# An attention kernel in quarter products: v joins the stream, first factors move into the attention

## The chip, the cores and the metric

The kernel runs on one core of a Trainium2 chip. A core has engines with a queue of instructions each: TensorE (PE, with weight loads listed as PEld), VectorE (DVE), ScalarE (ACT), GpSimd (POOL), and SyncE (SP), which only issues DMAs here. Engines wait for each other by semaphores. PE reads on-chip SBUF and writes PSUM; DVE and ACT read both, POOL only SBUF. The metric is device time in microseconds of one launch, all numbers in float32. The time before is 3212.28 us, the median of 3 runs (3211.11 to 3212.94).

## The reference

Two layers are applied one after the other to x of shape (8, 512, 32, 32): 8 images, C = 512 channels, N = 1024 tokens. A layer, for one image:

```python
xn = group_norm(x) * scale + bias          # 8 groups in layer 0, 32 in layer 1
q, k, v = split(qkv_w @ xn + qkv_b)        # (512, 1024) each, 8 heads of 64 channels
attn = softmax(q.T @ k / 8, over the keys) # per head, 1024 x 1024
out = proj_w @ (v @ attn.T) + proj_b + x
```

## The kernel before

The work is done in 16 units (u = 0 to 15): 8 images of layer 0, then 8 of layer 1. Layer 0 stores to mid in DRAM, from where layer 1 loads. The whole is an order written out by hand: each engine executes its instructions in program order, and hooks (lists of small steps, called `at("v", 6, ...)` or found by a step's number) say between which products a step is issued.

A unit has these stages on PE:

1. v (make_values): Winograd's form of Strassen's product, 7 outer products instead of 8, each of two 256-row chunks by direct matmuls: 56 matmuls of 128x256, tokens on the partitions. A float32 matmul is two instructions, each with a weight load, so 112.
2. q, k (make_pairs) and the projection of the unit before (project), in one stream (class Stream): here each of the 7 outer products is again done in Winograd's form, by 7 quarter products of 128x128 by 128x256. That is 49 matmuls, 98 instructions, for each of q, k and the projection. ACT copies the partial sum to the next quarter ("seed") and the seventh quarter product to SBUF ("late"); DVE finishes each outer product into running sums p1, u2, u3 and into the results; POOL adds the late part. The accumulators are two pairs of PSUM banks (apair), used in turn, with the other half of PSUM (sbank) for the partial sums.
3. The attention: 8 chunks (4 pairs of heads, 2 halves of the queries) of 8 steps each, s = 0 to 63. A step is 4 score matmuls of 64x64 tiles, exp on ACT, 4 matmuls with v, and on DVE one addition into the sums of p. Per chunk the sums are transposed and reduced on DVE, collected by small DMAs, inverted, spread by DMA (rb), and ao is multiplied by them (divide). There is no subtraction of a maximum.

A Winograd product needs left factors (of the weights, made once and stored as images in DRAM, loaded per unit in 7 pieces) and right factors of x. The class Right makes these: `mix(0..3)` makes the outer factors 5, 6, 4 and 7 by one DVE subtraction each, and `quarter` makes the inner factors t1, t2, t4 and b22 - b12 of one or two outer factors. For v only the outer factors are needed, so the inner ones are made by POOL during v. Their rooms are parts of the tiles for k, which are free then, and of others.

During the attention, the next unit's x is normalized in place. The function at_step is called behind each step with its number s. Its last part is one chain in which at most one arm runs in a step:

```python
if s == plan["norm"][0]:
    aggregate()
...
elif s in plan["apply"]:
    apply(*divmod(plan["apply"].index(s), NH))
elif s in (6 * NT + 2, 7 * NT + 3):
    right.mix(s // NT - 6)
```

NT is 8, NH 2, CC 4. In units other than 0 the plan is USUAL, whose apply steps are `[c * NT + t for c in range(2, 2 + CC) for t in (4, 6)]`; in unit 0 it is LATE, with 32, 33, 36, 38, 39, 41, 43, 44.

Since the softmax subtracts no maximum, the kernel guards itself: okay collects on DVE, with two instructions per pair of heads, whether all softmax sums lie between SUM_MIN = 2^-20 and SUM_MAX = 2^60, and asum whether ao is finite. At the end verdict reduces both over each partition, a matmul with ones counts the partitions in order, and the program reads this flag. If it is under 128, general_path (from line 1137) computes the whole output again, from x, in a loop over the 8 images with two layers each. It works plainly: for each of 64 blocks of 128 queries of a layer two matmuls of 512 columns for the scores, the maximum (line 1286), exp (1289), reciprocal and scaling (1291, 1292), 8 transposes on PE (1296), two copies from PSUM (1297), and per two blocks 8 matmuls with v of 256 columns (1303); before that 32 matmuls of 512 columns for v (1240) and 64 for q and k (1258), behind it 32 for the projection (1313). Scores, exponentials, transposed blocks and small results have two buffers each.

Of the kernel before, what the change touches and what calls it, by code (L numbers as in the profile page):

```python
# [11 lines left out]
F32 = mybir.dt.float32  # L12
I32 = mybir.dt.int32
AF = mybir.ActivationFunctionType
ALU = mybir.AluOpType
# [3 lines left out]
P = 128  # L19
# [13 lines left out]
def fast_path(ctx, tc, x, qkv_wT, proj_wT, vecs, groups, out, flag):  # L33
# [21 lines left out]
    def pool(name, bufs, **kw):  # L55
# [29 lines left out]
    okay = const.tile([P, 2 * BL], F32, name="okay")  # L85
# [6 lines left out]
    ot = aopool.tile([P, 3, 2, FD], F32, tag="ot", name="ot")  # L92

    images = [
        {
            sel: mids.tile([P, 7, FD if sel == "v" else 7 * P], F32, tag=f"i{sel}{l}", name=f"i{sel}{l}")
# [89 lines left out]
    def store_image(l, sel, left):  # L186
        to = images[l][sel]
        nc.sync.dma_start(to[:, :, :FD], left.block)
        if sel != "v":
            nc.sync.dma_start(to[:, :, FD:], left.made)  # L190

    def load_image(l, sel, slot, k):
        image = images[l][sel]
        return nc.sync.dma_start(slots[slot][:, k - 1, : image.shape[2]], image[:, k - 1, :])

    class Right:
# [24 lines left out]
        def quarter(self, pair, rooms, engine):  # L221
            v = self.views[pair[0]]
            t1, t2, t4 = rooms
            b11, b12, b21, b22 = (v[:, :, c, q, :] for c in range(2) for q in range(2))
            for i, k in enumerate(pair):
                self.inner[k] = {
                    1: b11[:, i], 2: b21[:, i], 3: b22[:, i], 7: b12[:, i],
                    5: t1[:, i], 6: t2[:, i], 4: t4[:, i],
                }
# [3 lines left out]
                partial(sub, b12, b22, b12),  # L233
# [162 lines left out]
    class Stream:  # L396
# [10 lines left out]
        def product(self, a, b, keep, finish):  # L407
# [6 lines left out]
            def part(j, dst, tile_name, bank, start=False):  # L414
                on(
                    "PE",
                    nc.tensor.matmul(dst, a[j], b[j], start=start, stop=j != 1, skip_group_check=True),  # L417
                    tile_name, bank,
                )
# [35 lines left out]

    def sum_steps(l, bias, name, early=None):
# [3 lines left out]
        def p1(main, m, late):  # L460
            t = st["p1"] = accpool.tile([P, 2, FD], F32, tag="acc", name=f"p1_{name}")
            on("DVE", nc.vector.tensor_scalar_add(t[:, 0, :], main[:, 0, :], vec[:, l, bias, 0:1]), m, 0)
# [14 lines left out]
        def u3(main, m, late):  # L477
            t = st["u3"] = accpool.tile([P, 2, FD], F32, tag="acc", name=f"u3_{name}")
            for i in range(2):
# [16 lines left out]
    def make_pairs(stream, w, sel, bias, left, early, hook):  # L496
# [32 lines left out]
        for k in ORDER:  # L529
# [7 lines left out]
            stream.product(left.quarters(k), w.right.inner[k], k == 3, finish)  # L537

# [67 lines left out]
    def make_values(w, left, banks, hook, between=None, behind=None):  # L606
# [3 lines left out]
        w.v = vpool.tile([P, NT, C], F32, tag="v", name=f"v_{u}")  # L610
        w.last["v"] = []
# [18 lines left out]
        run(steps[:6])  # L630
        if between is not None:
            between()
        run(steps[6:])
        if behind is not None:
            behind()
# [57 lines left out]
    def attention(w, at_step):  # L693
        u = w.u
        n_chunks = CC * NH
# [3 lines left out]

        def scores(s):  # L700
            c, t = divmod(s, NT)
            pr, qh = divmod(c, NH)
            if s < 6:
                bank = (*sbank, apair[1])[s % 3]
                before = state["exp"][s - 3 : s - 2] if s >= 3 else []
            elif s == n_steps - 1:
                bank = apair[0]
                before = state["free"][0]
            else:
                bank = sbank[s % 2]  # L710
                before = [state["exp"][s - (3 if s < 8 else 2)]]
            if s < 3:
                before = before + [i for i, _, _ in seen[("s0", "s1", "a1")[s]]]
# [17 lines left out]
        def products(s):  # L731
# [3 lines left out]
            banks = abank[2 * (c % 2) : 2 * (c % 2) + 2]  # L735
# [3 lines left out]
            if s == 0:  # L739
                before += w.last["v"] + [i for i, _, _ in seen["a0"]]  # L740
# [26 lines left out]
        def evacuate(c):  # L767
            pr, qh = divmod(c, NH)
            banks = abank[2 * (c % 2) : 2 * (c % 2) + 2]
            tmp = tmps[:, c % 2, :]  # L770
            i0 = nc.scalar.copy(tmp, banks[0])  # L771
# [8 lines left out]
        def reduced(c):  # L780
# [7 lines left out]
            if qh == NH - 1:  # L788
                lt = small.tile([BL, P // BL - 1, 2 * BL], F32, tag="lt", name=f"lt_{u}_{pr}")
                for k in range(1, P // BL):  # L790
                    nc.sync.dma_start(
                        lt[:, k - 1, :], red[k * BL : (k + 1) * BL].rearrange("i j h f -> i (j h f)")
# [3 lines left out]
        def reciprocals(pr):  # L796
            def work(name):
                return small.tile([BL, 2 * BL], F32, tag=name, name=f"{name}_{u}_{pr}", bufs=1)

            lt = state["lt"]  # L800
            one, two, tot, rows, rec = map(work, ("one", "two", "tot", "rows", "rec"))
            nc.vector.tensor_add(
                one, state["red"][:BL].rearrange("i j h f -> i (j h f)"), lt[:, 0, :]
            )
            nc.vector.tensor_add(two, lt[:, 1, :], lt[:, 2, :])
            nc.vector.tensor_add(tot, one, two)
            nc.vector.transpose(rows, tot)
            nc.vector.reciprocal(rec, rows)
            ok = okay[:BL]
            nc.vector.scalar_tensor_tensor(ok, tot, SUM_MAX, ok, ALU.is_le, ALU.mult)  # L810
            nc.vector.scalar_tensor_tensor(ok, tot, SUM_MIN, ok, ALU.is_ge, ALU.mult)
# [29 lines left out]
        for s in range(n_steps):  # L841
# [15 lines left out]
            summed(s, p)  # L857
# [3 lines left out]
        for h in range(NH):  # L861
            add_bias(CC - 2, h)
        transposed(n_chunks - 1)
        reduced(n_chunks - 1)
# [4 lines left out]

        w.finish = [partial(reciprocals, CC - 1), partial(divide, CC - 1), bias_last]  # L870
# [6 lines left out]
    nc.vector.memset(okay, 1.0)  # L877
# [33 lines left out]
    for u in range(2 * B):  # L911
        w = Unit()
        w.u, w.right, w.last, w.ready = u, right, {}, {}
# [11 lines left out]
        for sel in "qk":  # L925
            pairs = [
                qkpool.tile([P, 2, N], F32, tag=f"{sel}{r}", name=f"{sel}_{u}_{r}") for r in range(2)
            ]
            setattr(w, sel + "p", pairs)
            setattr(w, sel, [pairs[pr // 2][:, pr % 2, :] for pr in range(CC)])  # L930
# [18 lines left out]
        at("v", 1, make_rooms, partial(right.mix, 3))  # L949
# [448 lines left out]
```

## Time and profile before

| what | us |
|---|---|
| time, median of 3 | 3212.28 |
| the profiled execution | 3212.51 |
| its span | 3210.7 |
| PE busy | 3195.5 |
| DVE busy | 2773.0 |
| ACT busy | 1892.3 |
| POOL busy | 930.4 |
| the attention of unit 7 | 110.2 |
| v of unit 7 | 24.7 |
| q, k and projection of unit 7, together | 63.5 |

The page's busy times are sums over the execution; the span runs from the first to the last instruction. PE's share is 100%, but matmuls are pipelined and their ends modelled, so that a busy PE isn't PE at its peak. The prediction also uses three other views: busy time of each engine in a given stretch, the timeline (instructions in order of time, merged), and groups of instructions by line. The granted TensorE clock was 0.999 on average.

### The profile page before, as it was taken

How to read it: one execution, taken by the hardware profiler on the slowest of the kernel's cores; microseconds unless marked ns; L12 is line 12 of the kernel's file. 1: busy time of each engine (PE TensorE's matmuls, PEld its weight loads, DVE VectorE, ACT ScalarE, POOL GpSimd, SP SyncE). 2: the span in 40 equal slices, each digit the busy share in tenths (PEclk: the TensorE clock that was granted, in tenths of full speed). 3: DMA queues.
4: the chain of work that ended last, by engine and by line, in shares of the span. 5: the costliest groups of instructions: out<-in, count | busy, mean ns of one | idle time of the engine just before them, and what ended most of it. 6: DMA issues, size and time to landing. Idle time of an engine off the chain costs nothing.

```text
span 3210.7 us, 59813 instructions
## 1 busy us (share of the span) xinstructions
PE 3195.5 (100%) x23012; PEld 2023.7 (63%) x23012; DVE 2773.0 (86%) x3315; ACT 1892.3 (59%) x3077; POOL 930.4 (29%) x619
## 2 busy tenths in 40 slices
PE   9999999999999999999999999999999999999999
PEld 7466584765847658476584755747557485674843
DVE  7988988989899898888988889898888988989877
ACT  3656746466465665746657465574655746557464
POOL 5133060330604306043150421504224042240520
PEclk9999999999999999999999999999999999999999
DMA  5334242442534314233142332423323233232311
GB/s 197 109 108 131 79 159 96 132 131 93 160 105 128 120 45 157 74 108 127 43 162 68 107 124 61 143 70 122 108 79 126 74 119 106 86 130 74 123 64 49
DMA packets 151361, 344.84 MB, mean 107 GB/s; under 512 B 27168, under 2 KB 40992, under 8 KB 151072
## 3 DMA queue, kind: packets, MB, share of 16 engines
q1 hardware_dynamic: 150784, 340.81, 33.2%
q8 instruction: 187, 3.06, 0.4%
q14 instruction: 102, 0.84, 0.1%
q10 hardware_dynamic: 288, 0.13, 0.0%
HBM read 282.29 MB, written 57.02 MB: 106 GB/s over the span
## 4 chain that ended last, share of the span: by engine, by line
PE 94%; DVE 3%; issue 1%; POOL 0%; ACT 0%; DMA 0%; SPq 0%; DVEq 0%; POOLq 0%; ACTq 0%
PE a L746 26%; PE s L718 25%; PE s L417 18%; PE a L417 13%; PE a L394 6%; PE s L394 5%; DVE acc L765 1%; PE a L718 1%; PE s L672 0%; PE a L672 0%; DVE tr L777 0%; DVE acc L763 0%; DVE red L785 0%; DVE ao L772 0%; DVE xt L217 0%
## 5 line engine op out<-in xcount | busy, mean ns | idle before, releaser
L726 ACT ACTIVATE p<-s 128x1024 f32<-128x1024 f32 x976 | 997.6, 1024 | 522.7 <-PE s L718 495.4
L746 PE MATMUL a<-p,v 64*64 64x512 f32 x8192 | 1102.3, 589 | 0.0
L718 PE MATMUL s<-q,k 64*64 64x512 f32 x7808 | 1060.8, 590 | 0.0
L765 DVE TENSOR_TENSOR acc<-acc,p 128x1024 f32<-128x1024 f32 x768 | 938.3, 1222 | 77.9 <-ACT p L726 34.6
L746 PEld LDWEIGHTS a<-p,v 64*64 64x64 f32 x8192 | 385.1, 132 | 494.2 <-ACT p L726 348.3
L718 PEld LDWEIGHTS s<-q,k 64*64 64x64 f32 x7808 | 388.1, 133 | 426.9 <-issue 426.9
L422 ACT COPY a<-s 128x256 f32<-128x256 f32 x1308 | 465.8, 357 | 282.3 <-PE s L417 202.4
L947 POOL TENSOR_TENSOR k<-xn 128x512 f32<-128x512 f32 x16 | 20.3, 1269 | 1337.0 <-DVE xn L217 1337.0
L434 ACT COPY late<-s 128x256 f32<-128x256 f32 x327 | 121.7, 372 | 179.9 <-PE s L417 178.8
L394 PE MATMUL a<-w,xn 128*128 128x256 f32 x768 | 178.2, 382 | 0.5 <-DVE v L623 0.5
L832 ACT ACTIVATE ao<-ao,vec 128x512 f32<-128x512 f32 x128 | 88.4, 715 | 143.9 <-DVE ao L825 143.7
L394 PEld LDWEIGHTS a<-w,xn 128*128 128x128 f32 x768 | 144.6, 190 | 31.8 <-issue 12.2
L763 DVE TENSOR_TENSOR acc<-p,p 128x1024 f32<-128x1024 f32 x128 | 152.5, 1192 | 9.4 <-ACT p L726 9.4
L777 DVE STREAM_TRANSPOSE tr<-acc 128x1024 f32<-128x1024 f32 x128 | 158.0, 1235 | 0.0
L785 DVE TENSOR_REDUCE red<-tr 128x32 f32<-128x1024 f32 x128 | 154.3, 1206 | 0.6
L417 PE MATMUL s<-xn,w 128*128 128x256 f32 x492 | 146.8, 380 | 1.2 <-POOL xn L947 1.2
L417 PE MATMUL s<-k,w 128*128 128x256 f32 x492 | 146.4, 379 | 0.0
L417 PE MATMUL a<-xn,w 128*128 128x256 f32 x492 | 146.4, 379 | 0.0
L772 DVE TENSOR_TENSOR ao<-a,tmp 128x512 f32<-128x512 f32 x128 | 88.1, 688 | 61.4 <-ACT tmp L771 61.2
L417 PE MATMUL a<-xt,w 128*128 128x256 f32 x462 | 137.5, 379 | 0.0
L288 POOL TENSOR_TENSOR y<-var,half 128x4 f32<-128x4 f32 (+1 forms) x17 | 22.8, 1340 | 381.7 <-DVE var L286 381.7
L417 PE MATMUL s<-xt,w 128*128 128x256 f32 x432 | 128.5, 379 | 0.0
(204 smaller groups left out, 4685.9 us busy)
## 6 DMA issues: line engine op xcount, KB each, us to landing
w<-iq SPq DMA_DIRECT2D x105, 448.0 KB, 3.4
w<-ik SPq DMA_DIRECT2D x105, 448.0 KB, 5.8
w<-io SPq DMA_DIRECT2D x105, 448.0 KB, 3.4
rb<-drec SPq DMA_DIRECT2D x128, 256.0 KB, 3.9
w<-iv SPq DMA_DIRECT2D x105, 256.0 KB, 2.8
xn<-mid SPq DMA_DIRECT2D x36, 512.0 KB, 3.5
xn<-x_dram SPq DMA_DIRECT2D x32, 512.0 KB, 4.3
res<-x_dram SPq DMA_DIRECT2D x32, 512.0 KB, 6.5
```

Of the source, the lines that this page charges most:

```text
L394: step()
L417: nc.tensor.matmul(dst, a[j], b[j], start=start, stop=j != 1, skip_group_check=True),
L422: n = nc.scalar.copy(dst, one)
L434: on("ACT", nc.scalar.copy(late, seventh), s, 1)
L718: nc.tensor.matmul(bank[e * H : (e + 1) * H, j, :], w.k[pr][j * H : (j + 1) * H, t * P + e * H : t * P + (e + 1) * H], w.q[pr][j * H : (j ...
L726: exp = nc.scalar.activation(p, bank, AF.Exp, scale=SCALE)
L746: nc.tensor.matmul(banks[r][j * H : (j + 1) * H, :], w.v[rows, t, lo : lo + D], p[rows, j, :], start=(t == 0), stop=(t == NT - 1),)
L763: nc.vector.tensor_add(acc, state["first"], p)
L765: nc.vector.tensor_add(acc, acc, p)
L777: nc.vector.transpose(tr, state["acc"].pop(c))
L785: nc.vector.tensor_reduce(red[:, :, qh, :], state["tr"].rearrange("p j (f i) -> p j f i", i=BL), AX.X, ALU.add)
L832: nc.scalar.activation(cols, cols, AF.Identity, bias=vec[:, units[u][0], VB, pr : pr + 1])
```

## The change

In units 1 to 15 v is done in the stream as well, in 49 quarter products. Tokens have to be on the partitions, so x's factor is the weight and the left factor moves, with 128 columns: each quarter product is two matmuls. The images of v get their inner factors too (448 KB a piece for 256). Since v now needs the inner factors of x from its first product on, those of the outer factors 1 and 6 are made in the attention before on DVE, those of 2 and 3 by POOL at its end, and those of 5, 7 and 4 by POOL around the beginning of v. The last chunk's transpose and reduction move from the end of the attention into v; bias, divide and the factors of ao for the projection move to later products, some of them from DVE to POOL. The tiles of q and k are allocated once. PSUM pairs alternate with the unit's parity. The guard now keeps each unit's largest and smallest sum (extremes) and compares at the end. The reciprocals add the four rows by one reduction.

```diff
+        def single(self, k, rooms, engine, kept=None):
+            v, (t1, t2, t4) = self.outer[k], rooms
+            b11, b12, b21, b22 = (v[:, c, q * FD2 : (q + 1) * FD2] for c in range(2) for q in range(2))
+            b7 = b12 if kept is None else kept
+            self.inner[k] = {1: b11, 2: b21, 3: b22, 7: b7, 5: t1, 6: t2, 4: t4}
+            sub = engine.tensor_sub
+            return [
+                partial(sub, t1, b12, b11), partial(sub, t2, b22, t1), partial(sub, t4, b21, t2),
+                partial(sub, b7, b22, b12),
+            ]
...
-        def product(self, a, b, keep, finish):
+        def product(self, a, b, keep, finish, tokens=False):
...
+                for to, at, moving in (
+                    [(dst[:, ts(i, P)], b[j][:, ts(i, P)], a[j]) for i in range(2)]
+                    if tokens else [(dst, a[j], b[j])]
+                ):
...
+    def stream_values(stream, w, left, hook):
+        st, p1, u2, u3, wide = sum_steps(None, None, f"v_{w.u}")
...
+        for k in ORDER:
+            def finish(main, m, late, k=k):
+                steps[k](main, m, late)
+                hook("v", k)
+            stream.product(left.quarters(k), w.right.inner[k], k == 3, finish, True)
...
             nc.vector.reciprocal(rec, rows)
-            ok = okay[:BL]
-            nc.vector.scalar_tensor_tensor(ok, tot, SUM_MAX, ok, ALU.is_le, ALU.mult)
-            nc.vector.scalar_tensor_tensor(ok, tot, SUM_MIN, ok, ALU.is_ge, ALU.mult)
+            col = u * CC + pr
+            for i, op in enumerate((ALU.max, ALU.min)):
+                nc.vector.tensor_reduce(extremes[:BL, i, col : col + 1], tot, AX.X, op)
...
         evacuate(n_chunks - 1)
-        for h in range(NH):
-            add_bias(CC - 2, h)
-        transposed(n_chunks - 1)
-        reduced(n_chunks - 1)
+        summed(n_steps - 1, p)
+        w.sums = [partial(transposed, n_chunks - 1), partial(reduced, n_chunks - 1)]
...
+        else:
+            right.mix(3)
+            fifth = right.single(5, in_k((1, 1, 3), (1, 0, 0), (1, 0, 1)), nc.gpsimd)
+            run(fifth[:2])
+            run(right.single(7, in_k((1, 0, 2), (1, 0, 3), (1, 1, 2)), nc.gpsimd))
+            run(fifth[2:])
+            at("v", 6, partial(right.mix, 2), partial(run, right.single(4, in_k((1, 1, 0), (1, 1, 1), (0, 1, 3)), nc.gpsimd)))
...
+            transposed, reduced = old.sums
+            at("v", 1, transposed)
+            at("v", 2, reduced)
+            at("v", 4, reciprocals, old.bias_before)
+            at("v", 3, partial(ro.mix, 0), o_rooms)
+            at("q", 1, o_part(1, 0, 2))
+            at("q", 6, divide)
+            at("q", 2, bias_last, o_part(1, 2))
+            at("q", 7, partial(ro.mix, 1))
+            at("q", 4, partial(ro.mix, 3))
+            at("q", 3, partial(ro.mix, 2))
+            at("k", 1, o_part(5, 0, 2))
+            at("k", 6, o_part(5, 2))
+            at("k", 2, o_part(7), o_part(2, 0, 2))
+            at("k", 7, o_part(2, 2))
+            at("k", 4, o_part(4))
...
+        mixing = {}
+        if not last:
+            first_1 = right.single(1, [alone(w.kp[0], *at) for at in ((0, 0), (0, 1), (1, 0))], nc.vector)
+            first_6 = right.single(
+                6, [alone(w.kp[0], *at) for at in ((1, 1), (0, 2), (1, 2))], nc.vector, alone(w.kp[0], 0, 3)
+            )
+            mixing.update(zip((44, 46, 47, 52), first_1))
+            mixing.update(zip((54, 55, 59, 60), first_6))
+            mixing[43] = partial(right.mix, 0)
+            mixing[50] = partial(right.mix, 1)
+
+            def begin_high(right=right):
+                xa, xb = (ppool.tile([P, 2, FD], F32, tag="p", name=f"x{i}_{u + 1}") for i in "ab")
+                run(right.quarter((2, 3), (*halves(xa), halves(xb)[0]), nc.gpsimd, halves(xb)[1]))
...
             elif s in plan["apply"]:
                 apply(*divmod(plan["apply"].index(s), NH))
-            elif s in (6 * NT + 2, 7 * NT + 3):
-                right.mix(s // NT - 6)
+            elif s in mixing:
+                mixing[s]()
...
+        if not last:
+            begin_high()
...
+        for i, (bound, holds) in enumerate(((SUM_MAX, ALU.is_le), (SUM_MIN, ALU.is_ge))):
+            nc.vector.tensor_scalar(extremes[:, i, :], extremes[:, i, :], bound, None, holds)
+            nc.vector.tensor_reduce(low[:, i + 1 : i + 2], extremes[:, i, :], AX.X, ALU.min)
+        nc.vector.tensor_reduce(both, low, AX.X, ALU.min)
```

## The prediction

> **What bounds the kernel now.** I read the page first: the share of each engine and the chain of waits.
>
> ```profile
> span 3210.7 us, 59813 instructions
> PE 3195.5 (100%) x23012; PEld 2023.7 (63%) x23012; DVE 2773.0 (86%) x3315; ACT 1892.3 (59%) x3077; POOL 930.4 (29%) x619
> PE 94%; DVE 3%; issue 1%; POOL 0%; ACT 0%; DMA 0%; SPq 0%; DVEq 0%; POOLq 0%; ACTq 0%
> ```
>
> PE is busy throughout and carries 94% of the chain, so only fewer or shorter PE instructions, or new PE waits, can move the time. Then the busy time by stage of one unit (unit 7): attention, v, then q, k and projection. Columns: length, then busy time and instructions on PE, PEld, DVE, ACT, POOL, then clock, DMA share, GB/s.
>
> ```profile
> 1479.10:1589.30 110.20, 110.20 (x1033) 49.94 (x1032) 99.22 (x123) 76.27 (x83) 4.09 (x4) 1.00 0.25 77
> 1589.30:1614.00 24.70, 24.70 (x118) 21.69 (x115) 18.96 (x21) 5.53 (x8) 17.61 (x13) 1.00 0.40 134
> 1614.00:1635.20 21.20, 21.20 (x100) 18.55 (x99) 19.54 (x21) 12.24 (x35) 11.86 (x9) 1.00 0.53 153
> ```
>
> PE is full in all; DVE is at 90% in the attention, POOL at 71% in v. The records of v's matmuls start 0.2155 us apart. The price of a 128-column matmul comes from the idle products at the start, in the timeline (start, us, engine, line):
>
> ```profile
> 10.01 2.34 PE L330 MATMUL s<-gmat 128*128 128x128 f32 x10
> 12.14 1.54 PE L330 MATMUL s<-gmat 128*128 128x128 f32 x12
> ```
>
> In the first stretch they start 0.213 us apart, in the second 0.112 us, each with its own 128x128 weight load. Last the end of the timeline: the program ends with a flag, and after it nothing runs.
>
> ```profile
> 3204.59 0.19 PE L1133 MATMUL s<-ones,both 128*1 128x1 f32 x2
> 3204.82 0.15 ACT L1134 CAST flag<-s 1x1 int32<-1x1 f32 x1 [10.97 <-PE s L1133]
> ```
>
> So now the flag is 128, and the general path behind it is skipped.
>
> **The change does not issue all that it makes.** The new dictionary of steps holds 43, 44, 46, 47, 50, 52, 54, 55, 59, 60, but it is asked only in the last arm of an if/elif chain, behind the arm that normalizes x. That arm's steps are 8c+4 and 8c+6 for c = 2 to 5: 20, 22, 28, 30, 36, 38, 44, 46. Steps 44 and 46 are in both. From the attention of unit 1 on, the first two subtractions of x's block 1 (t1 = b12 - b11, t2 = b22 - t1) are never issued. In unit 0 the arm's steps include 43 and 44, so mix(0) (outer factor 5) and t1 are not issued there. Before, the two mixes stood at 50 and 59, in neither list.
>
> Their rooms then hold what was there: the unit's own k of channels 0 to 127, tokens 0 to 511. Three of block 1's seven inner products (5, 6, 4) get stale factors, and outer product 1 goes into all of q, k and v. I worked the two layers' arithmetic through on the reference's inputs with exactly these factors stale. The largest softmax sum of a unit, as a power of two, is 38, 32, 43 and 57 in units 1 to 4, 62 in unit 5, and rises to 90 in unit 15; with all factors made it is 11.5. The bound SUM_MAX is 60. The new test takes maxima per unit and compares them at the end. It fails from unit 5 on; up to 32 partitions give 0, the flag is under 128, and the general path computes the whole output again, after the fast path has run in full.
>
> **Time of the fast path.** The profiled execution took 3212.51 us, 0.2 over the median of 3212.28; 1.8 us lie around its span.
> - v on PE: 112 instructions x 0.2155 = 24.1 us become 49 quarter products x 2 halves x 2 passes = 196 x 0.112 = 22.0 us. 15 units: -33 us. This is on the path.
> - ACT: 7 products x 5 copies x 0.36 us (the COPY rows, 357 and 372 ns) = 12.6 us in v, as in q's stretch (12.24 of 21.20 us), where PE does not wait: 0.
> - DVE in v: 18.96 us, less divide and one outer mix (2.4), less some 2 of the reciprocals' small instructions, plus a copy (0.6) and 3.4 for the sums (0.7 + 5 x 1.22 + 4 x 0.68 = 9.5 for 5 x 1.22 before): 18.6 of 22 us. Hidden under PE. The divide, mixes and quarter steps of the projection that move on into q and k replace steps that moved from there to POOL. In the attention 6 issued steps of 128x256 (0.42 us by the 128x256 row of line 1015) are 2.5 us, against 3 sets of reciprocals shorter by 1 us: 99 of 110 us stays. If DVE's cover in the attention were gone, 2.5 x 15 = 38 us.
> - POOL in v: four 128x512 steps (6.5 us), twelve of 128x256 (0.73 to 0.88: 9.5 us) and six late additions (1.6: 9.6 us) are 25.6 us, more than the 22. The late addition of u2 queues behind the factors, and u3 on DVE, and through it PE's accumulators, wait for it. Between 0 (the spill lands in q's stretch, where POOL is 56% busy) and the whole excess of 3.6 us a unit, 54 us; I take 1 us a unit, as two PSUM pairs give a product of slack: +15 us.
> - DMAs on SP: v's seven images of 448 KB for 256 KB, one more 8 KB load a reciprocal; the share is 0.25 in the attention, landings are 3 to 6 us and issued 8 steps ahead: 0. The queue's packets fill 33.2% of the span by the page, so a delay of PE would need three times that.
> - The last pair's transpose and reduction (1.24 + 1.21 us) leave the end of the attention for v, with one more of the small loads on SP; reciprocals and their three DMAs follow at product 4, the divide at q's product 6. DMAs of this kind land in 3.9 us (rb's row), and two products, 6 us, lie in each gap: hidden. If a landing took 10 us, the divide would hold DVE for some 3 us, and q's sums behind it, 45 us in 15 units; nothing in the landings speaks for that, so it stays out of the bounds.
> - Unit 0's new order and the end's four more small instructions (0.16 us each): within 3 us either way; 0.
>
> Sum: 3212.5 - 33 + 15 = 3195 us, bounds 3177 (all of v's gain, 3 us more) to 3290 (POOL's 54 and DVE's 38 in full, v's gain gone). One rule speaks against the 0.112. The Trainium skill, "TensorE: Matmul & The Clock Gate", Part 3, says that a weight load overlaps running matmuls only in another row group, and its Part 2 puts a 128-column load at 107 ns; load plus matmul would be 0.22 us, and v 43 us, +280 us on the fast path by this estimate. The idle products load full rows and start every 0.112 us, so the row decides.
>
> **Time of the general path.** It has not run, so it is priced by like rows. It loops over 8 batches, two layers each. Per layer on PE:
> - 512-column matmuls: v 32, q and k 64, scores 64 blocks x 2, projection 32 = 256, two instructions each. In the last projection they start 0.43 us apart:
>
> ```profile
> 3201.50 0.19 PEld L672 LDWEIGHTS s<-ao,w 128*128 128x128 f32 x1 [0.24 <-issue]
> 3201.93 0.19 PEld L672 LDWEIGHTS s<-ao,w 128*128 128x128 f32 x1 [0.24 <-issue]
> ```
>
>   512 x 0.43 = 220 us.
> - transposes: 64 x 8 of 128x128, 1024 x 0.112 = 115 us at the price of a matmul.
> - weights on v: 256 of 256 columns, 512 x 0.2155 = 110 us.
>
> Sum 445 us a layer, 7.12 ms for 16. DVE per block: maximum 1.21, reciprocal 0.16, scaling 2 x 0.50, two copies 0.68 each = 3.7 us; x 64, with 37 us of the rest, 275 us a layer: hidden under PE if blocks overlap. ACT's exp, 1.02 x 64, is less. Before PE's first matmul of a layer the loads (4.3 us to landing) and the norm (8 x 0.68, some 16 x 0.16, and the first application) are 15 us: 16 x 15 = 240 us. So 7.36 ms, and with the fast path 3195 + 7360 = 10555 us, say 10550.
>
> Ends: below, all pairs of heads side by side on halves of the array (scores and weighted sums at half, -110 us a layer) and transposes at half (-57): 278 us a layer, then level with DVE: 7.9 ms in all. Above, no two blocks overlapping: scores 1.72 + maximum 1.21 + exp 1.02 + 1.16 + transposes 1.78 + copy 0.68 + 1 of handovers = 8.6 us x 64, with 257 for the rest = 807 us a layer: 16.3 ms. I take PE's sum: two heads stand next to each other in the code and each pool there has two buffers, so one's PE work covers the other's DVE chain. The Trainium skill, same page, Part 1, says that PE falls to half its clock after some 3.4 us idle; the first stretch of idle products shows half rate. If that held throughout, the 7.12 ms would double, 17.7 ms in all, by this estimate.
>
> **Rivals.**
> - The branch is not taken: the sums stay under 2^60, the stale factors notwithstanding. Then the time is the fast path's, 3195 us, faster by 0.5%. It decides from the largest sum: 2^60 against 2^62 to 2^90 in eleven units. That margin and the arithmetic speak against it.
> - The branch is not taken and POOL's queue in v sets the pace: 54 us of waits less 33: 3234 us, slower by 0.7%. For it, 25.6 us of work in 22; against it, the slack in q.
> - The general path runs without overlap: 16.3 ms. Against it the two buffers.
>
> **How the numbers follow.** Chances: general path runs 0.88 (10.55 ms; inside 8.5 to 13 ms 0.82, outside 0.06, the serial form included); fast path alone and faster 0.08; alone and within 0.2% (what a measurement here can tell from nothing, 6 us) 0.01; alone and slower 0.03. Faster 0.08, same 0.01, slower 0.91. The range is 8500 to 13000 us: three quarters of the way from 10550 to the lower end, four tenths of it to the upper.
>
> **What will show it.** Instructions of the general path (reciprocals on 128x1, maxima, table loads) after the flag, and a span over 8 ms; in the attention two 128x256 subtractions fewer than the eight listed; v's matmuls 0.112 us apart, 196 of them in 22 to 24 us; the clock at 1.0 in the loop, PE over 85% busy there. Wrong if the span ends at the flag; if v takes over 25 us; if the loop takes over 1.2 ms or under 0.7 ms a batch, where I have 0.92.

## The result, and the profile after

| | us | ratio to before, 95% interval |
|---|---|---|
| before | 3212.6 | |
| changed kernel | 10768.7 | 3.352 [3.346, 3.358] |

The profiled execution of the changed kernel took 10768.74 us. Its page gives the span, and the busy time, share of the span and instructions of each engine:

```profile
span 10766.9 us, 123912 instructions
PE 10139.9 (94%) x48912; PEld 5562.2 (52%) x48912; DVE 6705.5 (62%) x9538; ACT 3392.1 (32%) x5796; POOL 1140.0 (11%) x835
```

Before there were 23012 PE instructions. Where nearly all of the other 25900 come from is seen in the timeline at the place where the kernel ended before (start, us, engine, line):

```profile
3322.81 0.19 PE L1255 MATMUL s<-ones,both 128*1 128x1 f32 x2
3323.03 0.15 ACT L1256 CAST flag<-s 1x1 int32<-1x1 f32 x1 [8.99 <-PE s L1255]
3326.00 0.35 SPq L1291 DMA_DIRECT2D gvec<-vecs_dram  x1
3326.12 0.20 POOL masks.py:197 MEMSET gident<- 128x128 f32 x1 [137.93 <-DMA out_dram<-xn]
```

The flag is read, and then the loads of the general path begin: the branch is taken. So the time has two parts, split at the flag's row: the fast path, 3323 us (3205 before), and the general path, 10766.9 - 3323.0 = 7443.9 us. The second is 98% of what was lost. Its costliest groups (engine, operation, tiles, shapes, count, then busy us, mean ns, and idle time before):

```profile
L1403 PE MATMUL gs<-gk,gq 64*128 64x512 f32 x4096 | 2102.6, 643 | 127.0 <-ACT gp L1411 122.2
L1425 PE MATMUL gpav<-gpts,gv 128*64 128x256 f32 x8192 | 1950.8, 386 | 46.2 <-DVE gpts L1419 46.2
L1418 PE MATMUL gpt<-gident,gp 128*128 128x128 f32 x8192 | 1179.5, 296 | 99.9 <-DVE gp L1414 87.1
L1414 DVE TENSOR_SCALAR gp<-gp,grsum 128x1024 f32<-128x1024 f32 x1024 | 753.4, 746 | 13.5
```

And one of its eight passes, the third (columns as before: length, busy time and instructions of PE, PEld, DVE, ACT, POOL, then clock, DMA share, GB/s):

```profile
5168.00:6093.00 925.00, 864.40 (x3081) 435.71 (x3079) 488.54 (x779) 168.37 (x279) 0.00 (x0) 0.96 0.01 5
```

PE is busy for 864 of 925 us, DVE for 489, so the blocks do overlap and PE sets the pace. The granted clock is 0.96 there, where I had expected 1.0.

The missing factors show in the attention. From 1956.6 to 2068 us line 1234, which executes the dictionary's steps on DVE, has six subtractions of 128x256 where eight are listed (count: durations in ns, first and last start):

```profile
L1234 DVE TENSOR_TENSOR k<-xt x2: 418/952/1487, 2054.4 to 2065.2; 128x256 f32<-128x256 f32 x2
L1234 DVE TENSOR_TENSOR k<-xt,k x2: 417/418/418, 2055.8 to 2062.6; 128x256 f32<-128x256 f32 x2
L1234 DVE TENSOR_TENSOR k<-xn,k x1: 419/419/419, 2041.0 to 2041.0; 128x256 f32<-128x256 f32 x1
L1234 DVE TENSOR_TENSOR xn<-xn x1: 415/415/415, 2050.0 to 2050.0; 128x256 f32<-128x256 f32 x1
```

The first of these rows also holds a 1487-ns execution of a 418-ns instruction; that is the thread to the other loss.

**The fast path is slower too**, by 118 us. Between the first score matmuls of successive attentions lie 204.6 to 205.1 us in the later units (198.5 to 198.6 before) and 205 to 209 us up to unit 5 (198.7 to 200.2). That is +63 us for units 6 to 15, +42 for units 1 to 5 and +13 for unit 0. In unit 10, 4.4 us of 6.2 are lost in v and 1.8 in q and k, where one seed stands behind ACT's two bias additions (a gap of 0.68 us between the starts of PE's instructions) and one behind DVE's factors of the projection, which come late (1.77 us). The windows of the attention before unit 10's v, and of that v, which starts at 2066.8:

```profile
1956.60:2066.80 110.20, 110.20 (x1033) 49.85 (x1032) 100.42 (x120) 76.30 (x83) 7.80 (x7) 1.00 0.28 90
2066.80:2073.00 6.20, 4.13 (x36) 3.72 (x32) 6.10 (x5) 1.44 (x4) 6.12 (x4) 1.00 0.00 1
2073.00:2076.10 3.10, 1.52 (x10) 1.52 (x11) 3.06 (x4) 1.50 (x4) 0.34 (x1) 0.87 0.00 0
2076.10:2079.20 3.10, 3.10 (x18) 3.10 (x18) 2.00 (x3) 1.09 (x3) 2.62 (x4) 0.58 0.00 0
2079.20:2095.95 16.75, 16.52 (x144) 16.25 (x143) 11.23 (x16) 10.45 (x28) 11.64 (x12) 1.00 0.02 4
```

PE is full to the last microsecond of the attention, waits in v's first stretches, and then has a stretch at a granted clock of 0.58. What it waits for is in the waits of v, PE alone (waited for: us, times, longest):

```profile
PE s L435 <- ACT a L443: 3.9, 3, 3.1
```

It waits for ACT's seed. ACT's timeline says what the seed waits for:

```profile
2070.18 0.36 ACT L443 COPY a<-s 128x256 f32<-128x256 f32 x1
2074.17 0.63 ACT L443 COPY a<-s 128x256 f32<-128x256 f32 x2 [3.63 <-DVE ao L858]
```

That is the last evacuation of the attention: v's second product puts its seed into the PSUM pair that still holds the last chunk's accumulators. DVE's and POOL's timelines around it (a row may hold several executions, x2):

```profile
2060.16 2.54 DVE L848 TENSOR_TENSOR acc<-acc,p 128x1024 f32<-128x1024 f32 x2
2062.95 2.32 DVE L848 TENSOR_TENSOR acc<-acc,p 128x1024 f32<-128x1024 f32 x1
2066.60 2.28 DVE L906 SCALAR_TENSOR_TENSOR ao<-ao,rb 128x1024 f32<-128x1024 f32 x1
2073.39 0.69 DVE L858 TENSOR_TENSOR ao<-a,tmp 128x512 f32<-128x512 f32 x1
```

```profile
2064.26 2.13 POOL L408 TENSOR_TENSOR xa<-xn,xa 128x512 f32<-128x512 f32 x1
2066.48 1.33 POOL L408 TENSOR_TENSOR xb<-xn,xa 128x512 f32<-128x512 f32 x1
2067.77 2.25 POOL L408 TENSOR_TENSOR xb<-xn 128x512 f32<-128x512 f32 x1
```

POOL starts its factors for v at 2062.92, in the attention's last 4 us. From there on a sum, 1.22 to 1.27 us before, takes 2.32, the divide 2.28 rather than 1.22, and two of POOL's own four steps 2.13 and 2.25 rather than 1.27. DVE, at 100.4 of 110.2 us, has no room for it: the evacuation ends at 2074.1, 7.3 us behind the start of v. (Of the last chunk's evacuation DVE now also does the copy, 0.68 us, which ACT did before.) In the kernel before it ended 2.8 us behind the start of the v shown in the prediction, and that v's second product went to another bank.

### The profile page after: what moved, and what is told of

It is laid out like the page before. It is cut to its first block, busy times and chain, and to the rows that moved or that the text cites. A ratio compares the mean times of both kernels' runs of the same rounds, so it can differ in the third digit from the quotient of the medians.

```text
span 10766.9 us, 123912 instructions
## 1 busy us (share of the span) xinstructions
PE 10139.9 (94%) x48912; PEld 5562.2 (52%) x48912; DVE 6705.5 (62%) x9538; ACT 3392.1 (32%) x5796; POOL 1140.0 (11%) x835
## 5 line engine op out<-in xcount | busy, mean ns | idle before, releaser
L1411 ACT ACTIVATE gp<-gs,gnmax 128x1024 f32<-128x1024 f32 x1024 | 1141.4, 1115 | 4719.6 <-DVE gnmax L1408 3548.3
L1403 PE MATMUL gs<-gk,gq 64*128 64x512 f32 x4096 | 2102.6, 643 | 127.0 <-ACT gp L1411 122.2
L1425 PE MATMUL gpav<-gpts,gv 128*64 128x256 f32 x8192 | 1950.8, 386 | 46.2 <-DVE gpts L1419 46.2
L1425 PEld LDWEIGHTS gpav<-gpts,gv 128*64 128x64 f32 x8192 | 1067.0, 138 | 1135.9 <-DVE gpts L1419 304.0
L1419 DVE COPY gpts<-gpt 128x512 f32<-128x512 f32 x2048 | 1301.7, 683 | 477.7 <-PE gpt L1418 464.7
L1408 DVE TENSOR_REDUCE gnmax<-gs 128x1 f32<-128x1024 f32 x1024 | 1242.1, 1218 | 554.2 <-PE gs L1403 553.9
L1418 PEld LDWEIGHTS gpt<-gident,gp 128*128 128x128 f32 x8192 | 968.6, 150 | 623.6 <-DVE gp L1414 299.1
L1418 PE MATMUL gpt<-gident,gp 128*128 128x128 f32 x8192 | 1179.5, 296 | 99.9 <-DVE gp L1414 87.1
L1380 PE MATMUL gpqk<-gxn,gwqkv 128*128 128x512 f32 x2048 | 920.0, 599 | 0.0
L1414 DVE TENSOR_SCALAR gp<-gp,grsum 128x1024 f32<-128x1024 f32 x1024 | 753.4, 746 | 13.5
L443 ACT COPY a<-s 128x256 f32<-128x256 f32 x1728 | 614.7, 357 | 463.0 <-PE s L435 264.9
```

Source lines behind the costliest of these rows:

```text
L1380: nc.tensor.matmul(ps, wqkv[l][:, c, o : o + P], xn[c][:, ts(h, FD)], start=(c == 0), stop=(c == CC - 1),)
L1403: nc.tensor.matmul(s[:, ts(h, FD)], q[rows, ts(i, P)], k[rows, ts(h, FD)], start=True, stop=True,)
L1408: nc.vector.tensor_reduce(nmax, s, AX.X, ALU.max, negate=True)
L1411: nc.scalar.activation(p, s, AF.Exp, bias=nmax, accum_out=sums)
L1414: nc.vector.tensor_scalar_mul(p, p, rsum)
L1418: nc.tensor.transpose(pt[:, ts(t, P)], p[:, ts(g * KT + t, P)], ident)
```

## The experiments

The theory had two parts. (A) The collision of the step numbers leaves factors stale, the softmax sums pass 2^60, and the general path runs. (B) On the fast path, which I had forecast 18 us faster than before, the loss of 118 us comes from POOL beside DVE at the border between attention and v.

**e1_fix: the steps get a test of their own.**

```diff
             elif s in plan["apply"]:
                 apply(*divmod(plan["apply"].index(s), NH))
-            elif s in mixing:
+            if s in mixing:
                 mixing[s]()
```

> The steps of the dictionary mixing are asked for in an if of their own, behind the chain, so that steps 43, 44 and 46 are issued. Theory A (two or three factors are never made, the softmax sums leave the range, the flag sends the program into the general path): the program ends at the flag. The fast path of the changed kernel took 3323 us to the flag; two more subtractions of 0.42 us in 14 attentions, where DVE is late at the end already, add up to 12 us: 3325 to 3340 us, 3% to 4% slower than before. Rival R1 (the new range test with its extremes is what fails, whatever the factors): the general path runs still, 10770 to 10790 us.

Measured: 3338.5 us, ratio 1.0392 [1.0374, 1.0409]. The last row of its timeline is the flag:

```profile
3331.94 0.15 ACT L1256 CAST flag<-s 1x1 int32<-1x1 f32 x1 [8.91 <-PE s L1255]
```

One word undone, and 7430 us are gone; nothing else of the change was touched. (A) is shown, and with it that the new way of testing the ranges is not the cause. (B) is seen without the general path: the change as it was meant is 3.9% slower than before.

**e2_loose: the stale factors kept, the bound raised.**

```diff
-SUM_MIN, SUM_MAX = 2.0**-20, 2.0**60
+SUM_MIN, SUM_MAX = 2.0**-20, 2.0**120
```

> The changed kernel with SUM_MAX 2^120 for 2^60; the skipped factors stay stale, so this leaves out two subtractions a unit and its q, k and v are not the reference's. Theory A: largest sum 2^90, so the flag holds and the program ends behind the fast path, 3323 + 2 = 3325 us. Rival R2 (not the sums but values that are not finite, in asum, trip the flag): the general path runs, 10770 us.

Measured: 3329.3 us (one run); the flag is at 3321.56 and nothing runs behind it. So the largest sum lies between 2^60 and 2^120 and is no infinity; the arithmetic in the prediction had 2^90. The time is also the changed kernel's own fast path, without the general one.

**e3_forced: the kernel before, made to take the general path.**

```diff
-SUM_MIN, SUM_MAX = 2.0**-20, 2.0**60
+SUM_MIN, SUM_MAX = 2.0**-20, 2.0**5
```

> The kernel before with SUM_MAX 2^5, so that its sums of 2^10 to 2^11.5 are out of range: the general path alone is added to the fast path before. Theory A: 3212 + 7440 (10767 less 3323, from the profile after) = 10650 us, within 30. Rival R3 (the general path is slow only because of what the changed fast path leaves, such as a lower clock): well under 10600 us.

Measured: 10611.6 us (one run), the flag at 3205.33, so the general path takes 10609.7 - 3205.3 = 7404 us there and 7444 in the changed kernel. The general path has a price of its own, and the change has no part in it but for 40 us. Of these, 30 are PE's busy time (6932 us against 6902, for the same 24640 instructions), at a mean granted clock of 0.95 against 0.96; what lowers the clock stays open.

**e4_gated: POOL's factors held back.** In e1_fix, the first of POOL's four factor steps waits for the last evacuation.

```diff
-                run(right.quarter((2, 3), (*halves(xa), halves(xb)[0]), nc.gpsimd, halves(xb)[1]))
+                steps = right.quarter((2, 3), (*halves(xa), halves(xb)[0]), nc.gpsimd, halves(xb)[1])
+                follows(steps[0](), old.freed, "behind the last accumulators")
+                run(steps[1:])
```

> As e1_fix, and POOL's first subtraction for factors 2 and 3 waits for the copy of the last accumulators by DVE. In the profile after, PE stands 3.4 us in v's second product for that copy (it ends 7.3 us behind the attention's last matmul; 2.1 us in the kernel before), and then runs at half clock for about 3.5 us. W1 (POOL's subtractions double the length of DVE's additions beside them, 1.22 to 2.3 us, and so make the copy late): the copy ends 4 us behind the matmuls, the wait of 3.4 us goes to under 1 us, the half clock with it; POOL's factors come some 3 us later and cost back 1 to 3 us: 2 to 5 us a unit less than e1_fix, 3250 to 3300 us. W2 (DVE's queue is long by its own added work: two first factors, the divide, the second copy): the copy stays over 6 us behind, and POOL's delay is added: 3330 to 3390 us.

Measured: 3323.6 us, ratio 1.0350 [1.0333, 1.0368]. DVE's timeline at the end of unit 9's attention (v starts at 2057.74):

```profile
2054.69 1.22 DVE L848 TENSOR_TENSOR acc<-acc,p 128x1024 f32<-128x1024 f32 x1
2056.16 1.22 DVE L907 SCALAR_TENSOR_TENSOR ao<-ao,rb 128x1024 f32<-128x1024 f32 x1
2060.48 0.69 DVE L858 TENSOR_TENSOR ao<-a,tmp 128x512 f32<-128x512 f32 x1
```

Without POOL beside them the same instructions take 1.22 us, and the evacuation ends 3.4 us behind v's start. So the mechanism of (B) is there. But of the gain only 15 us is left, a time in neither theory's range, since v now waits for POOL itself. PE's longest waits in that v:

```profile
PE s L435 <- POOL k L408: 1.5, 1, 1.5
PE s L435 <- POOL xb L408: 1.4, 1, 1.4
PE s L435 <- ACT a L443: 0.7, 2, 0.5
```

**e5_spread and e6_both: less for DVE at the border, without and with the gate.** From e1_fix, the applications of x's normalization move from steps 20 to 46 to 20 to 32, the eight factor steps from 44 to 60 to 43 to 57, the mixes from 43 and 50 to 26 and 34, and the divide of the third pair of heads moves into v.

```diff
-        "apply": [c * NT + t for c in range(2, 2 + CC) for t in (4, 6)],
+        "apply": (20, 21, 22, 24, 28, 30, 31, 32),
...
+            at("v", 5, old.before)
...
+            at_1, at_6, at_0, at_low = (
+                ((44, 46, 47, 52), (54, 55, 59, 60), 43, 50) if u == 0
+                else ((43, 44, 46, 47), (49, 51, 56, 57), 26, 34)
+            )
```

> As e1_fix, with DVE's extra work taken from the last two chunks of the attention: x is normalized at steps 20 to 32 for 20 to 46, the mixes stand at 26 and 34 for 43 and 50, the eight first subtractions at 43 to 57 for 44 to 60, and the third divide moves from step 61 to v's product 5. POOL starts as in e1_fix, so its steps still stretch DVE's. W1 (POOL's stretching alone makes the copy late): DVE has some 4 us less in its queue, the copy still lies 5 us behind, the wait in the second product is about 1.5 us, and without the half clock behind it v takes 26 us for 29: 3338 - 45 = 3290 us. W2 (DVE's queue counts as much): the copy is under 4 us behind, v takes 24 us: 3265 us. If the length of DVE's queue doesn't matter: 3338 us.

> e5_spread with e4_gated: POOL waits for the last copy. DVE is free, so the copy ends 1.5 us behind the attention, and POOL starts 1.5 us earlier than in e4_gated, 4 us later than in e5_spread. W3 (POOL's chain of factors is what v waits for next; in e4_gated its waits are 0.5, 1.7, 1.7 and 0.6 us a unit): some 2 us of these stay, v takes 25 us, 3280 us, not faster than e5_spread. If DVE's and POOL's mutual stretching is all: v takes 23 us, 3250 us, faster than e5_spread.

Measured: e5_spread 3281.7 us, ratio 1.0215 [1.0198, 1.0232]; e6_both 3320.1 us, 1.0338 [1.0321, 1.0356]. The evacuation in e5_spread, on DVE's timeline (unit 10's v starts at 2040.31):

```profile
2041.94 0.69 DVE L858 TENSOR_TENSOR ao<-a,tmp 128x512 f32<-128x512 f32 x1
```

It ends 2.3 us behind the start of v, though the two sums ahead of it still take 2.1 us each beside POOL: the length of DVE's queue counts as well as the stretching. Moving DVE's work out of POOL's way is worth 57 us, almost half of the loss. With the room made, the gate costs 38 us, where neither theory had it cost anything. In unit 10 POOL's chain begins 6.4 us later and v is 3.0 us longer; 1.6 us of that are PE's waits for POOL's factors, of which e5_spread has none there. So in this kernel what has to give way at the border is DVE, not POOL.

**e7_split and e8_tuned: the small waits of the stream.** These kernels still carry e6_both's gate. In e7_split the four bias additions of 0.7 us on ACT (two in v and two in q), which held up seeds, are issued one per product, the projection's factor steps on DVE are spread over k, and v's first product does its seventh quarter before it needs the second seed.

```diff
-            at("q", 2, bias_last, o_part(1, 2))
-            at("q", 7, partial(ro.mix, 1))
+            at("q", 2, partial(old.add_bias, CC - 1, 1), o_part(1, 2))
+            at("q", 7, partial(old.add_bias, CC - 1, 0), partial(ro.mix, 1))
...
-            at("k", 2, o_part(7), o_part(2, 0, 2))
+            at("k", 2, o_part(5, 2, 3), o_part(2, 0, 2))
```

> e6_both with four small moves against the other waits that e1_fix shows in each unit: ao's factors spread evenly over k's products (PE stands 1.77 us in k where DVE has five subtractions stretched from 0.42 to 1.4 us by POOL beside them); the bias additions on ACT one by one (0.5 us in v, 0.68 in q, where two hold up the seeds); in v's first product the seventh quarter product goes ahead of the sixth (0.78 us for the first seed, 0.45 of it filled). Sum 1.8 + 1.2 + 0.45 = 3.4 us a unit, 52 us: e6_both less 52. If the k wait isn't DVE's stretched work: only 25 less.

Measured: 3277.6 us, ratio 1.0205 [1.0188, 1.0222]: 42.5 us less than e6_both.

In e8_tuned, the left factors of layer 0's projection are made by POOL behind unit 0's k. In the changed kernel DVE made them in k, and stood there for a load of that weight:

```profile
87.49 1.42 DVE L408 TENSOR_TENSOR w<-w 128x512 f32<-128x512 f32 x2 [12.54 <-DMA w<-proj_wT_dram]
```

```diff
-            outer_o, inner_o = mix_left(slot_q)
-            at("k", 2, partial(run, outer_o[:2]))
-            at("k", 7, partial(run, outer_o[2:]))
...
+            outer_o, inner_o = mix_left(slot_q, nc.gpsimd)
+            at("k", 3, partial(run, outer_o), partial(run, inner_o))
```

> e7_split, and in unit 0 POOL makes the projection's left factors behind k for DVE within k. In the profile after, DVE stands 12.5 us there for the four loads of these weights (issued when q's slot comes free, landing 14 us later), and PE 10.8 us behind it. Ten to twelve us less than e7_split, at the risk that POOL's eight long steps (2 us) stretch DVE in unit 0's attention: then 0 to 5 less.

Measured: 3270.1 us, ratio 1.0189 [1.0172, 1.0206], 7.5 us less. Unit 0's q and k go from 51.0 to 38.0 us (37.8 before), 13 us; 4 us of it come back in unit 0's attention, where the eight POOL steps now lie beside the sums.

**e9_ungated and e10_bias_in_q.** e9_ungated is e8_tuned without the gate; in e10_bias_in_q the other two bias additions leave v for q.

```diff
-            at("v", 4, reciprocals, partial(old.add_bias, CC - 2, 0))
-            at("v", 3, partial(ro.mix, 0), o_rooms, partial(old.add_bias, CC - 2, 1))
+            at("v", 4, reciprocals)
+            at("v", 3, partial(ro.mix, 0), o_rooms)
-            at("q", 1, o_part(1, 0, 2))
+            at("q", 1, partial(old.add_bias, CC - 2, 1), o_part(1, 0, 2))
+            at("q", 5, partial(old.add_bias, CC - 2, 0))
```

> e8_tuned without the wait that holds POOL's factors behind the last evacuation; everything else is kept. W4: the wait's cost (3320.1 against 3281.7, 38 us) and the gains of the small moves (42.5 and 7.5 us) lie in different products and add up: 3281.7 - 42.5 - 7.5 = 3232 us, v at 23.8 to 24.3 us in the units from 6 on. W5: without the wait the DVE sums beside POOL's subtractions take 2.1 to 2.2 us again, and v's second product, which the small moves do not touch, waits for the last evacuation in the units 1 to 5 and 11: about half of the 38 us stays lost, 3250 us.

> e9_ungated with the two bias additions of the third chunk moved out of v: one behind q's first product, one behind its fifth. In the spread version the 24th gap of v (1.2 to 1.8 us in every unit) waits for a seed that stands behind these two ScalarE additions of 0.7 us, which wait for the divide. W6: that wait goes and nothing takes its place in q: -1.1 us in each of 15 units, 15 to 20 us less than e9_ungated, 3212 to 3217 us, within 0.2% of before. W7: the seeds of q's products then stand behind the additions, one wait of 0.3 to 0.6 us per addition: 5 to 10 us less than e9_ungated only.

Measured: 3229.5 us, ratio 1.0057 [1.0040, 1.0074], and 3219.2 us, 1.0022 [1.0012, 1.0031]. The parts do add up (3232 expected), but v's second product does wait in units 1 to 5 and 11, as the rival had it. The bias additions gave 10 us: W6's mechanism at W7's size, since in e9_ungated the wait was 0.7 to 0.9 us in seven units only, and 0.3 to 0.5 in the other eight (PE's row in unit 10 reads "[0.33 <-ACT a L443]"). In two units only did a wait in q, of 0.5 us, take its place. In the later units v has come close to what it can be: 22.8 us for 196 instructions (196 x 0.1117 = 21.9), with one last 0.33-us gap at each of the first two seeds. A unit then takes 197.0 us against 198.5 before. In units 1 to 5, and for a shorter time in unit 6, the old wait is there (ACT's timeline in unit 5; v starts at 1007.98):

```profile
1011.22 0.36 ACT L443 COPY a<-s 128x256 f32<-128x256 f32 x1 [0.57 <-PE s L435]
1014.19 0.63 ACT L443 COPY a<-s 128x256 f32<-128x256 f32 x2 [2.62 <-DVE ao L862]
```

Units 2 to 5 follow the attentions in which DVE also makes layer 1's weight images, eight subtractions of 0.7 to 1.1 us each, and unit 1 the one with POOL's eight steps. That these steps are the reason is likely but not shown: no run takes layer 1's away, and unit 6 waits without them.

**e11_evacuate_first: the evacuation ahead of two sums.** In units 0 to 4 only.

```diff
-            if s < n_steps - 1:
+            if s < n_steps - 1 - held:
                 summed(s, p)
             at_step(s, state)
         products(n_steps - 1)
         evacuate(n_chunks - 1)
-        summed(n_steps - 1, p)
+        for s in range(n_steps - 1 - held, n_steps):
+            summed(s, state["p"][s])
```

> e10_bias_in_q with one edit: in the attentions of the units 0 to 4 the sums of the third and second last steps are issued behind the last evacuation, so that VectorE takes the accumulators out of PSUM about 4 us earlier; no work is added or left out. Theory: what still holds v's second product in the units 1 to 5 (a gap of 2.4 to 2.6 us in each) is that evacuation alone, so the gap goes: v of these units from 26.9 to about 24 us, 5 x 2.5 = 12 to 15 us off, 3204 to 3208 us. Rival: the sums that now come behind delay v's own combinations on VectorE and the tiles that POOL writes into, and the wait comes back at a later product: less than 5 us off.

Measured: 3217.2 us, ratio 1.0016 [1.0007, 1.0026], within the uncertainty of e10_bias_in_q's. ACT's and DVE's timelines in the same unit (v starts at 1006.52):

```profile
1017.26 0.36 ACT L443 COPY a<-s 128x256 f32<-128x256 f32 x1 [3.13 <-DVE p_v L498]
```

```profile
1007.53 0.69 DVE L863 TENSOR_TENSOR ao<-a,tmp 128x512 f32<-128x512 f32 x1
1008.14 6.74 DVE L853 TENSOR_TENSOR acc<-acc,p 128x1024 f32<-128x1024 f32 x3
1014.80 1.75 DVE L218 TENSOR_TENSOR xn<-xn 128x1024 f32<-128x1024 f32 x1
1016.47 0.68 DVE L498 TENSOR_TENSOR p_v<-a,late 128x512 f32<-128x512 f32 x1
```

The evacuation is 4.4 us earlier, and the gap at the second product is gone. In units 2 to 5 the same 2.5 us come back at a later product, which waits for DVE's first combination of v behind three sums of 2.1 to 2.3 us. The rival is right: it is DVE's backlog that costs, and reordering it only moves the place where PE meets it.

**e12_first_images: unit 0's eight factor steps from POOL to DVE, spread over the attention.** q's images for unit 1 share the room and are loaded later.

```diff
-            outer_o, inner_o = mix_left(slot_q, nc.gpsimd)
-            at("k", 3, partial(run, outer_o), partial(run, inner_o))
...
+        if u == 0:
+            making = [part for parts_of in mix_left(slot_q) for part in parts_of]
+            made = 0, "o", slot_q
...
-            n, odd = divmod(s - NT, 2)
+            n, odd = divmod(s - (NT if u else 5 * NT + 2), 2)
```

> e11_evacuate_first, and the projection's left factors of layer 0 (eight subtractions that POOL makes beside VectorE's sums in the first attention) are made by VectorE one by one in the chunks 1 to 4 of that attention; q's images for unit 1 are loaded later in it, since they share the room. If POOL's subtractions are what holds unit 0's attention at 114.7 us (110.5 before), it falls to about 111 us: 3 to 4 us less than e11_evacuate_first, 3200 to 3205 us, faster than before by 0.2 to 0.4%. If VectorE's load is what counts, whoever makes the factors, it stays at 114 to 115 us and the time is that of e11_evacuate_first.

Measured: 3218.6 us, ratio 1.0020 [1.0011, 1.0029], the time of e11_evacuate_first. Unit 0's attention takes 114.3 us (116.5 in e11_evacuate_first, 114.7 in e10_bias_in_q, 110.5 before). The time is the rival's, but the trace does not decide for it: of the two waits in that attention (3.4 us together in e11_evacuate_first, none before) one of 2.1 us is left, and behind it the windows of PE (length, PE's busy time and instructions, clock) show half the clock:

```profile
146.40:149.60 3.20, 3.20 (x20) 0.53 0.00 0
```

So POOL's subtractions did hold up one wait. What holds the other is not shown.

No version beats the kernel before. From e1_fix to e11_evacuate_first 121 us came back, without any change in the amount of PE's work: both have 24272 PE instructions.

## Why the prediction was right or wrong

- **The branch: right.** "The general path behind it is skipped" became "runs" for the reason given; e1_fix and e2_loose show both halves of it, the collision and the size of the sums.
- **The general path: 7360 forecast, 7444 measured (7404 in the kernel before): right, but as near as that by luck, since errors cancel.** By line and layer (the groups' busy time over 16): scores 131 us for 110, weights on v 122 for 110, v, q, k and projection 116 for 110, transposes 74 for 115. A transpose is one instruction here, 512 a layer of 0.144 us; I had priced two of 0.112. A pass has 60 us in which PE is idle, where I had 30. The bounds from both sides were far too wide for how well PE covers DVE: 489 of 925 us.
- **128-column matmuls at 0.112 us: right.** v's instructions start 0.1117 us apart wherever nothing waits and the clock is 1.0. The Trainium skill, "TensorE: Matmul & The Clock Gate", Part 3, has a weight load overlap running matmuls only in another row group or in a background weight buffer; v's loads all take full rows, and at this pace they show no such wait. But v was to gain 2.2 us a unit, 33 in all, and the units of e10_bias_in_q with the fewest waits are 1.5 us shorter, which would be 22 in all: two seeds have no product to lie behind, 0.7 us. In the changed kernel itself v takes 29.2 us in unit 10 and over 28 in every unit: my own sign of being wrong, "if v takes over 25 us", came true, and not because of the price of a matmul.
- **The fast path: wrong.** 3195 was forecast, at most 3290; it took 3325 with what lies around the span. The bound was also added up wrongly: 3212.5 + 54 + 38, with v's gain gone, is 3305, and that too was passed. Three terms failed.
  - *"Hidden under PE" and "99 of 110 us stays", of DVE.* I summed DVE's work over v and over the attention. What counts is where it stands at the end, when the accumulators have to be out. The step at 60, the divide and the sums stood there, and e5_spread got 57 us back by moving them away.
  - *"I take 1 us a unit, as two PSUM pairs give a product of slack", of POOL.* I asked what POOL's own 25.6 us would make wait, and not what they do to DVE's instructions beside them. In unit 10 two sums, the divide and a factor step lost 1.1 us each, and a third sum 0.3. And the slack was not there: v's second product now takes the pair of the last chunk, where v before took another bank. No run gave it another bank again, so what the shared pair alone costs stays open.
  - *"Unit 0's new order ... within 3 us".* It was 13 us, one load that DVE stood waiting for. I had not looked at when the projection's first weights land.
- **What I left out of the sum**: the half-rate stretch behind such a wait (in unit 10, 18 instructions in 3.1 us, where 28 fit at 0.1117), and ACT's bias additions between q's and v's seeds.
- **The rival "POOL's queue in v sets the pace", 3234 us**, had the right engine, and only the gated kernels, e4_gated to e8_tuned, look like it: in e4_gated PE waits 3.4 us of one v for POOL. In the changed kernel the wait was DVE's, stretched by POOL.

With the general path at 70% of the time, the miss of 130 us on the fast path was 1.2% of the total. As a forecast of what the change does once its steps are all issued, it would have had the wrong sign.

## What to carry to other kernels

When steps are entered by number into an if/elif chain, list the numbers of every arm first; steps that are never issued cost 7.4 ms here, and no wait in the profile would have pointed to it. When work moves to an idle engine, look at what its neighbour does in those microseconds, and judge an engine's cover at the moment a buffer has to be free, not by its share of the stage. And before splitting a product finer for PE, count the handovers it adds: 1.5 us of gain in a 198-us unit is used up by one late evacuation.

## What the runs showed of the hardware

**DVE and POOL slow each other when both read two operands from SBUF.** A 128x1024 sum takes 1.22 us alone and mostly 2.1 to 2.3 beside POOL; POOL's 128x512 subtraction takes 1.27 alone and 2.1 to 2.25 beside DVE; a 0.42-us subtraction on DVE took 1.49. The kernel before had it already: on POOL's timeline in unit 7's v, three of the 128x512 steps took 2.2 to 2.3 us, each beside a DVE instruction with two operands in SBUF, and the others 1.27, some of them beside DVE's additions from PSUM. One of the three:

```profile
1604.69 2.30 POOL L947 TENSOR_TENSOR xn<-xn 128x512 f32<-128x512 f32 x1
```

An addition with one operand in PSUM, the evacuation's, kept its 0.69 us beside POOL in e10_bias_in_q. e4_gated shows the cause by taking POOL away. The Trainium skill, "SBUF — State Buffer", section "SBUF: two separate sides", has the rule: GpSimd and a VectorE instruction with two SBUF inputs share one pair of ports, and whoever starts first holds it for its whole instruction. These numbers agree with it; I had not weighed it.

**A wait of 2 us can halve the clock for 3 us, or not.** The same wait in unit 0's attention, once in e10_bias_in_q and once in e11_evacuate_first. First PE's timeline and the windows of the one:

```profile
148.88 1.09 PE L833 MATMUL a<-p,v 64*64 64x512 f32 x8 [1.99 <-ACT p L813]
```

```profile
147.00:150.40 3.40, 1.52 (x16) 1.00 0.00 0
150.40:153.60 3.20, 3.20 (x32) 1.00 0.02 5
```

Then of the other (length, PE's busy time and instructions, clock):

```profile
148.67 1.09 PE L834 MATMUL a<-p,v 64*64 64x512 f32 x8 [1.99 <-ACT p L814]
```

```profile
147.00:150.40 3.40, 1.73 (x16) 0.94 0.00 0
150.40:153.60 3.20, 3.20 (x20) 0.53 0.02 5
```

At 0.53 of the clock PE does 20 instructions in 3.2 us rather than 32, so the second wait cost 3.2 us and the first 2.0. The Trainium skill, "TensorE: Matmul & The Clock Gate", Part 1, has the clock set by a window of 3.4 us that runs freely; two waits of one length with two outcomes fit that, and here a PE wait of 2 us cost between 2.0 and 3.2 us.
